# The last three queries put off, and attention's gathers held to the fourth maximum of a step

## The chip, the cores and the metric

The kernel runs on one core of a Trainium2 chip. The metric is the device time of one launch in microseconds (us), lower is better. All numbers are float32.

## The reference

64 sequences of 64 tokens with 512 features pass four layers, each added to its input: x = x + layer(x).

- Layer 0: a dense layer of 512 x 512 whose weight and bias are picked for each sequence out of 16.
- Layer 1: a dense layer of 512 x 512, the same for all, and a rank-16 adapter picked for each sequence out of 8.
- Layer 2: attention against a cache of keys and values. q has 8 heads, k and v have 4, of 64 features. q and k are normed (root mean square over the 64 features of a head, with a learned gain) and rotated by the position. k and v are written into a paged cache at the sequence's position; every query sees the last 256 positions.

```python
q = _rope(_rms(q, q_norm_scale), pos)
...
scores = einsum('bghtd,bgsd->bghts', qg, k_all) * SCALE
p = softmax(where(allowed, scores, -inf), axis=-1)
o = einsum('bghts,bgsd->bghtd', p, v_all)
return einsum('bto,do->btd', o, Wo)
```

- Layer 3: a 64 x 64 product over the tokens of a sequence, with weight and bias picked out of 8.

## The kernel before

**Tiles and phases.** The 4096 tokens are 32 tiles (NT) of 128 tokens, two sequences each. The engines' orders are written out by hand: each engine runs its instructions in the order in which the Python program names them, and semaphores join the engines. The first phase (to about 519 us of the span) does layers 0 and 1 for all tiles, the keys and values (stored to `kvd` in DRAM), and the queries of the first 25 tiles (stored turned to `qTd`). The last eight tiles (LATE) keep their layer-1 output, turned, in SBUF.

**The passage.** In lines 975 to 992 GpSimd starts the gathers of tiles 0 and 1 (`load_kv`), and a loop over tiles 25 to 30 makes their queries: `product` (L140, four float32 matmuls, shown as eight), ScalarE's square (L120), VectorE's sum (L122), ScalarE's root (L123), VectorE's reciprocal and scaling (L126, L128), VectorE's rotation with cosine and sine gains (L133 to L135, the work of `turned`), then `turn_q` (L174: TensorE transposes the query, ScalarE copies it to `qTs`, SP stores it). The query of tile 31 is made in step 0.

**A step.** Then come 32 steps. Step s holds, in this order on each engine:

- GpSimd: `load_kv(s + 2)`: five indirect gathers (L787), 128 rows of 2 KB each, into `kv` (four buffers). In steps 0 and 1 a copy of one element (`after_keys`) makes them wait for the keys of tile s. Then `add_one(s - 2)` (L833), a small sum into the weight `w3`.
- `scores(s)`: 8 products (L860, `ps`), each followed by one VectorE operation that adds the mask, flips the sign and takes the maximum of a row (L868, `mx`; four for the first pair of heads, `gp` 0, then four for the second), and ScalarE's exponential with its sum (L872).
- `attend(s - 1)`: 48 matmuls (L907, `po`), VectorE copies the result (L925).
- `normalise(s, ...)`: VectorE's reciprocals and 8 scalings (L880, L884).
- `last(s - 4)` in even steps from 4 on: layer 3 of two tiles (L947, `pz`; ScalarE L954).
- `project(s - 2)`: the output projection (L935, `py`, in the one bank of pool `pyp`) and VectorE's sum (L939).
- `keys(s + 1)`: TensorE transposes the gathered keys (L841, L847), ScalarE copies them to `kT` (L842, L848).
- `turn(s)`: TensorE transposes the probabilities (L893, L897, `ppt`); VectorE copies two of the five results to `pT` (L894), ScalarE the three others (L894, L898).

All PSUM results but `py` share a ring of seven banks, so a new product waits until the bank used seven allocations earlier has been copied out. The tiles of a `kv` buffer are free again when `attend` has read them, so that a gather for tile i waits for `attend(i - 4)`.

**Who waits.** SP's queue issues the loads of masks, queries, layer-3 weights and the stores in program order. GpSimd's queue is in order as well: what stands behind a waiting gather waits with it.

Of the kernel before, what the change touches and what calls it, by code (L numbers as in the profile page):

```python
# [12 lines left out]
F32 = mybir.dt.float32  # L13
# [36 lines left out]
LATE = 8  # L50
# [9 lines left out]
def body(ctx: ExitStack, tc: tile.TileContext, a: dict, out: bass.AP):  # L60
# [54 lines left out]

    def turned(ps, n, to, pool, X, kind, cg, sg):

        psv = ps[:, : n * HD].rearrange("p (h d) -> p h d", d=HD)
        sq = pool.tile([128, n, HD], F32, name=f"sq{kind}", bufs=2)
        S.activation(sq, psv, AF.Square)  # L120
        ss = pool.tile([128, n], F32, name=f"ss{kind}", bufs=2)
        V.tensor_reduce(ss, sq, AX.X, ALU.add)  # L122
        S.activation(ss, ss, AF.Sqrt, bias=epst, scale=1.0 / HD)  # L123
        yield
        rs = pool.tile([128, n], F32, name=f"rs{kind}")
        V.reciprocal(rs, ss)  # L126
        qn = pool.tile([128, n, HD], F32, name=f"qn{kind}", bufs=2)
        V.tensor_tensor(qn, psv, bc(rs[:, :, None], [128, n, HD]), ALU.mult)  # L128
        yield
        t2 = sq  # L130
        for f in range(2):
            fs, of = slice(f * HALF, (f + 1) * HALF), slice((1 - f) * HALF, (2 - f) * HALF)
            V.tensor_tensor(t2[:, :, fs], qn[:, :, of], bc(sg[:, None, fs], [128, n, HALF]), ALU.mult)  # L133
        V.tensor_tensor(qn, qn, bc(cg[:, None, :], [128, n, HD]), ALU.mult)  # L134
        X.tensor_tensor(to, qn, t2, ALU.add)  # L135
# [6 lines left out]

    def parts_q(i, pq, X, cs=None):
        qr = late.tile([128, H, HD], F32, name="qr", bufs=2)
        qrs[i] = qr.rearrange("p h d -> p (h d)")
        return turned(pq, H, qr, late, X, 0, *(cs or gains(0, i, late, X)))

# [22 lines left out]
    def turn_q(i, pool=late):  # L170
        qrf = qrs.pop(i)
        pqt = bank("pqt")
        for c in range(KC):
            TE.transpose(pqt[:, c * 128 : (c + 1) * 128], qrf[:, c * 128 : (c + 1) * 128], ident)  # L174
        qT = pool.tile([128, 2, 2, 2, T], F32, name="qTs", bufs=2 if pool is late else 4)
# [604 lines left out]

    kvs, kTs, mbs, prs, pTs, oTs, qTs, pairs, x3s = {}, {}, {}, {}, {}, {}, {}, {}, {}

# [8 lines left out]

    def after_keys(i):

        seen = bp.tile([1, 1], F32, name="seen")
        P.tensor_copy(seen, kTs[i][0:1, 0, 0:1])

# [53 lines left out]
    def scores(i):  # L850
        kT, mb, qT = kTs.pop(i), mbs.pop(i), qTs.pop(i)
        pr = bp.tile([128, G, 2 * NPOS], F32, name="pr")
        mx = bp.tile([128, G, 2], F32, name="mx")
        sm = bp.tile([128, G, 2], F32, name="sm")
        for gp in range(2):
            for b2 in range(2):
# [8 lines left out]
                for g2 in range(2):  # L865
# [3 lines left out]
                        out=p, in0=ps[g2][:, :NPOS], in1=mb[:, b2, :], scale=-1.0, scalar=3.0e38,  # L869
                        op0=ALU.add, op1=ALU.min, accum_out=mx[:, g, b2 : b2 + 1],  # L870
                    )
                    S.activation(  # L872
                        p, p, AF.Exp, bias=mx[:, g, b2 : b2 + 1], scale=-1.0, accum_out=sm[:, g, b2 : b2 + 1],
                    )
# [99 lines left out]

    for i in range(2):
        load_kv(i)
    load_q(0)
    load_mask(0)

    parts = {}  # L980
    for i in range(NT - LATE + 1, NT - 1):
        pq = product(i, wq, "pq")
        parts[i] = parts_q(i, pq, V, cs[i])
        next(parts[i])
        if i > NT - LATE + 2:
            turn_q(i - 2, bp)
        if i - 1 in parts:
            run(parts.pop(i - 1))
        next(parts[i])
    keys(0)  # L990
    load_q(1)
    load_mask(1)
    wo = bp.tile([128, KC, D], F32, name="wo", bufs=1)
    for s in range(NT):
        if s + 2 < NT:
            if s < 2:
                after_keys(s)
            load_kv(s + 2)
            load_mask(s + 2)
        if s and s + 2 < NT:  # L1000
            load_q(s + 2)
        scores(s)
        if s >= 2:
            add_one(s - 2)
        if s:
            load_pair(s - 1)
            attend(s - 1)
        else:

            parts[NT - 1] = parts_q(NT - 1, product(NT - 1, wq, "pq", pyp), V, cs[NT - 1])  # L1010
            turn_q(NT - 3, bp)
        if s == 2:
            next(parts[NT - 1])
        normalise(s, 0)
        normalise(s, 1)
        if s % 2 == 0 and s >= 4:
# [79 lines left out]
```

## Time and profile before

| what | value |
|---|---|
| median of 3 runs | 972.71 us (970.54 to 973.45) |
| profiled execution, its own time | 976.14 us |
| its span | 974.3 us |
| granted TensorE clock, mean | 0.995 |
| 0 to 500 us: TensorE busy | 484.42 of 500.00 |
| 545 to 558: TensorE busy, clock | 12.99 of 13.00, 1.00 |
| 558 to 580: TensorE busy, clock | 15.96 of 22.00, 0.84 |
| 580 to 640: TensorE busy, VectorE, ScalarE, GpSimd | 58.01, 43.95, 33.76, 25.60 of 60.00 |
| 820 to 880: the same | 58.32, 43.18, 38.05, 23.21 of 60.00 |
| DMA engines' mean share, 820 to 880 | 0.63 |

Times within the profile count from the span's start. A line such as `kv<-kvd,idxn` names what is written and what is read; in brackets stand the engine's idle time just before and what ended it. Matmuls are pipelined: their starts are measured, their ends modelled.

### The profile page before, as it was taken

What the parts mean: (1) busy time and instruction counts of PE and PEld (TensorE: products, weight loads), DVE (VectorE), ACT (ScalarE), POOL (GpSimd) and SP (SyncE); (2) the same over time, 40 slices, a digit from 0 to 9 for tenths busy, and PEclk for the clock granted to TensorE, in tenths of its full rate; (3) what the DMA queues carried; (4) which work ended last, traced back from release to release, by engine and by line L of the source; (5) the groups of instructions that cost most, each with busy time, mean ns of one, the idle gap of its engine ahead of it and who ended that gap; (6) DMA issues with size and microseconds to landing.
All of it is one profiled execution on the core that took longest, in us unless ns stands there. A gap on an engine that the chain in (4) does not pass through costs nothing.

```text
span 974.3 us, 17800 instructions
## 1 busy us (share of the span) xinstructions
PE 936.3 (96%) x5407; PEld 509.6 (52%) x5407; DVE 608.0 (62%) x1734; ACT 405.2 (42%) x1081; POOL 404.6 (42%) x604
## 2 busy tenths in 40 slices
PE   8899998999999999999999979999999999999998
PEld 3344444444444444444344546766666666666665
DVE  5746788888572353532316768666667776666673
ACT  1212122322232222232223656655566666665663
POOL 4344355554453454534425433334444333334400
PEclk9999999999999999999999989999999999999999
DMA  8898999999999999999854774666665565666621
GB/s 305 306 317 311 358 360 322 395 367 363 381 333 391 393 320 392 359 376 397 310 216 155 241 240 134 205 205 203 204 193 193 177 201 184 190 197 196 198 72 45
DMA packets 132944, 260.74 MB, mean 268 GB/s; under 512 B 32481, under 2 KB 41186, under 8 KB 132850
## 3 DMA queue, kind: packets, MB, share of 16 engines
q1 hardware_dynamic: 108722, 178.74, 51.2%
q0 software_dynamic: 23232, 79.71, 24.6%
q10 hardware_dynamic: 896, 1.16, 0.3%
q8 instruction: 43, 0.70, 0.3%
q14 instruction: 51, 0.42, 0.1%
HBM read 190.06 MB, written 69.50 MB: 266 GB/s over the span
## 4 chain that ended last, share of the span: by engine, by line
PE 70%; DVE 3%; DMA 1%; issue 1%; ACT 1%; SPq 0%; POOL 0%; DVEq 0%; ACTq 0%
PE py L935 12%; PE po L907 8%; PE ps L860 8%; PE p L655 7%; PE pk L140 7%; PE ppt L893 6%; PE pq L140 6%; PE p L266 6%; PE pkt L841 2%; PE ppt L897 2%; PE pkt L847 1%; PE pz L947 1%; DMA w<-in_W 1%; PE pqt L174 1%; DVE pT L894 1%
## 5 line engine op out<-in xcount | busy, mean ns | idle before, releaser
L787 POOL DMA_INDIRECT kv<-kvd,idxn x128 | 126.3, 987 | 216.8 <-PE po L907 159.6
L872 ACT ACTIVATE pr<-pr,mx 128x320 f32<-128x320 f32 x256 | 140.1, 551 | 6.9 <-DVE mx L868 2.6
L266 PE MATMUL p<-w,xt 128*64 128x512 f32 x512 | 122.1, 610 | 1.3 <-DMA w<-in_W 1.3
L935 PE MATMUL py<-wo,oT 128*128 128x512 f32 (+1 forms) x264 | 118.3, 591 | 1.7 <-DVE qn L128 1.7
L140 PE MATMUL pk<-wkv,x 128*128 128x512 f32 x256 | 117.2, 603 | 0.6 <-ACT x L676 0.6
L155 POOL DMA_INDIRECT st<-in_kvc,cidx x68 | 67.3, 990 | 109.2 <-DMA kvd<-st 98.6
L655 PE MATMUL p<-w,x 128*128 128x512 f32 x256 | 112.5, 596 | 0.1
L140 PE MATMUL pq<-wq,x 128*128 128x512 f32 x248 | 111.3, 593 | 0.0
L868 DVE CUSTOM_DVE_ANT_0 pr<-ps,mb 128x320 f32<-128x320 f32 x256 | 107.8, 486 | 5.5 <-PE ps L860 2.7
L860 PE MATMUL ps<-kT,qT 64*128 64x320 f32 x512 | 88.1, 460 | 13.6 <-DVE pT L894 8.5
L894 DVE COPY pT<-ppt 128x512 f32<-128x512 f32 x64 | 41.8, 687 | 77.6 <-PE ppt L893 33.7
L290 DVE TENSOR_TENSOR x<-pt,x 128x512 f32<-128x512 f32 x32 | 22.0, 688 | 107.1 <-PE pt L289 94.7
L884 DVE TENSOR_SCALAR pr<-pr,sm 128x320 f32<-128x320 f32 x256 | 85.2, 394 | 2.2
L907 PE MATMUL po<-pT,kv 128*64 128x128 f32 (+1 forms) x1536 | 84.7, 282 | 1.6 <-issue 1.6
L907 PEld LDWEIGHTS po<-pT,kv 128*64 128x64 f32 (+1 forms) x1536 | 71.0, 138 | 22.3 <-DVE mx L868 13.6
L935 PEld LDWEIGHTS py<-wo,oT 128*128 128x128 f32 x264 | 47.5, 189 | 61.6 <-issue 58.4
L655 PEld LDWEIGHTS p<-w,x 128*128 128x128 f32 x256 | 47.8, 190 | 58.3 <-issue 56.5
L135 POOL TENSOR_TENSOR qr<-qn,sq 128x512 f32<-128x512 f32 x25 | 31.7, 1267 | 109.8 <-DVE qn L134 109.8
L266 PEld LDWEIGHTS p<-w,xt 128*64 128x64 f32 x512 | 35.9, 138 | 71.1 <-issue 65.5
L140 PEld LDWEIGHTS pk<-wkv,x 128*128 128x128 f32 x256 | 46.9, 192 | 49.9 <-issue 48.5
L123 ACT ACTIVATE ss<-ss,epst 128x4 f32<-128x4 f32 (+1 forms) x64 | 19.2, 299 | 125.3 <-DVE ss L122 124.5
L860 PEld LDWEIGHTS ps<-kT,qT 64*128 64x128 f32 x512 | 45.5, 185 | 45.0 <-DVE pT L894 24.0
(200 smaller groups left out, 1344.2 us busy)
## 6 DMA issues: line engine op xcount, KB each, us to landing
w<-in_W SPq DMA_DIRECT2D x62, 1024.0 KB
kvd<-st SPq DMA_DIRECT2D x68, 512.0 KB
xt<-in_xT SPq DMA_DIRECT2D x32, 256.0 KB
x2d<-x2n SPq DMA_DIRECT2D x32, 256.0 KB
kvd<-kvn SPq DMA_DIRECT2D x32, 256.0 KB
qTd<-qTs SPq DMA_DIRECT2D x32, 256.0 KB
qT<-qTd SPq DMA_DIRECT2D x32, 256.0 KB
x2r<-x2d SPq DMA_DIRECT2D x32, 256.0 KB
```

Of the source, the lines that this page charges most:

```text
L140: TE.matmul(ps, x2s[i][:, c, :], w[:, c, :], start=c == 0, stop=c == KC - 1)
L155: P.indirect_dma_start(out=st, out_offset=None, in_=a["kvc"].rearrange("(n r) d -> n (r d)", r=2), in_offset=bass.IndirectOffsetOnAxis(ap= ...
L266: TE.matmul(p0[hs, :], xs[i][:, c, hs], w0s[i][h][:, c, :], start=c == 0, stop=c == KC - 1)
L655: TE.matmul(p1[i], x1s[i][:, c, :], w1[:, c, :], start=c == 0, stop=False)
L787: P.indirect_dma_start(out=kv[:, n, :], out_offset=None, in_=kvd, in_offset=bass.IndirectOffsetOnAxis(ap=at, axis=0),)
L860: TE.matmul(ps[g2][:, :NPOS], qT[rows, gp, b2].rearrange("p h t -> p (h t)"), kT[rows, gp, b2 * NPOS : (b2 + 1) * NPOS], start=True, stop= ...
L868: V.tensor_tensor_reduce(out=p, in0=ps[g2][:, :NPOS], in1=mb[:, b2, :], scale=-1.0, scalar=3.0e38, op0=ALU.add, op1=ALU.min, accum_out=mx[ ...
L872: S.activation(p, p, AF.Exp, bias=mx[:, g, b2 : b2 + 1], scale=-1.0, accum_out=sm[:, g, b2 : b2 + 1],)
L884: V.tensor_scalar(p, p, sm[:, g, b2 : b2 + 1], None, ALU.mult)
L893: TE.transpose(pt[:, n * 128 : (n + 1) * 128], pr[:, g, at : at + 128], ident)
L907: TE.matmul(po[b2][g2 * 64 : (g2 + 1) * 64, gp * 128 : (gp + 1) * 128], kv[rows, n, (G + g) * HD : (G + g + 1) * HD], pT[rows, c, m * 128 ...
L935: TE.matmul(py[:, fs], oT[:, c].rearrange("p b t -> p (b t)"), wo[:, c, fs], start=c == 0, stop=c == KC - 1,)
```

## The change

It has three parts.

- The queries of tiles 29 to 31 (LAST on) are no longer normed and rotated in the passage. ScalarE copies their products out of PSUM into `raw` (the product of 29 between `keys(0)` and `scores(0)`, those of 30 and 31 in steps 0 and 1). GpSimd squares them in steps 2 to 4, VectorE sums the squares in steps 3 to 5, ScalarE takes all three roots in step 6 and runs one exponential behind them, VectorE takes the reciprocal, GpSimd scales and rotates in steps 7 to 12, and `turn_q` follows in steps 9, 11 and 13. The rotation of tile 28 moves from VectorE to GpSimd.
- The gathers of three tiles (15, was 10) start ahead of the passage's loop. From step 1 on `load_kv(s + 2)` stands behind `scores(s)` and behind a one-element copy that reads the fourth maximum (`after_scores`); the maxima get one tile for each pair of heads, so that the copy waits for the first four operations alone. `after_keys` goes.
- GpSimd's other work of a step, `add_one` and the squares and rotations, stands behind the gathers. `qTs` has three buffers in the passage where it had four.

```diff
-    def turned(ps, n, to, pool, X, kind, cg, sg):
+    def turned(ps, n, to, pool, X, kind, cg, sg, M=V):
...
-            V.tensor_tensor(t2[:, :, fs], qn[:, :, of], bc(sg[:, None, fs], [128, n, HALF]), ALU.mult)
-        V.tensor_tensor(qn, qn, bc(cg[:, None, :], [128, n, HD]), ALU.mult)
+            M.tensor_tensor(t2[:, :, fs], qn[:, :, of], bc(sg[:, None, fs], [128, n, HALF]), ALU.mult)
+        M.tensor_tensor(qn, qn, bc(cg[:, None, :], [128, n, HD]), ALU.mult)
...
-    def after_keys(i):
+    def after_scores(i):
 
         seen = bp.tile([1, 1], F32, name="seen")
-        P.tensor_copy(seen, kTs[i][0:1, 0, 0:1])
+        P.tensor_copy(seen, mxs[i][0][0:1, 1, 1:2])
...
-        mx = bp.tile([128, G, 2], F32, name="mx")
+        mxs[i] = [bp.tile([128, 2, 2], F32, name=f"mx{gp}") for gp in range(2)]
...
-    for i in range(2):
+    for i in range(3):
         load_kv(i)
...
+    def keep_raw(i, pq):
+        S.copy(raw[:, i - LAST].rearrange("p h d -> p (h d)"), pq)
+
+    def rotate_raw(i, part):
+        x, t2, (cg, sg) = raw[:, i - LAST], sqr[:, (i - LAST) % 2], cs[i]
+        if part == 0:
+            P.tensor_tensor(x, x, bc(ssr[:, i - LAST, :, None], [128, H, HD]), ALU.mult)
+            for f in range(2):
+                fs, of = slice(f * HALF, (f + 1) * HALF), slice((1 - f) * HALF, (2 - f) * HALF)
+                P.tensor_tensor(t2[:, :, fs], x[:, :, of], bc(sg[:, None, fs], [128, H, HALF]), ALU.mult)
+        else:
+            P.tensor_tensor(x, x, bc(cg[:, None, :], [128, H, HD]), ALU.mult)
+            P.tensor_tensor(x, x, t2, ALU.add)
+            qrs[i] = x.rearrange("p h d -> p (h d)")
...
-    for i in range(NT - LATE + 1, NT - 1):
-        pq = product(i, wq, "pq")
-        parts[i] = parts_q(i, pq, V, cs[i])
+    for i in range(NT - LATE + 1, LAST):
+        X = P if i == LAST - 1 else V
+        parts[i] = parts_q(i, product(i, wq, "pq"), X, cs[i], X)
...
+    run(parts.pop(LAST - 1))
     keys(0)
+    keep_raw(LAST, product(LAST, wq, "pq"))
+    turn_q(LAST - 2, bp)
     load_q(1)
     load_mask(1)
...
         if s + 2 < NT:
-            if s < 2:
-                after_keys(s)
-            load_kv(s + 2)
             load_mask(s + 2)
         if s and s + 2 < NT:
             load_q(s + 2)
         scores(s)
+        if s and s + 2 < NT:
+            after_scores(s)
+            load_kv(s + 2)
         if s >= 2:
             add_one(s - 2)
+        if 2 <= s <= 4:
+            x = raw[:, s - 2]
+            P.tensor_tensor(sqr[:, s % 2], x, x, ALU.mult)
+        elif 7 <= s <= 12:
+            rotate_raw(LAST + (s - 7) // 2, (s - 7) % 2)
         if s:
             load_pair(s - 1)
             attend(s - 1)
-        else:
-            parts[NT - 1] = parts_q(NT - 1, product(NT - 1, wq, "pq", pyp), V, cs[NT - 1])
-            turn_q(NT - 3, bp)
-        if s == 2:
-            next(parts[NT - 1])
+        if s < 2:
+            keep_raw(LAST + 1 + s, product(LAST + 1 + s, wq, "pq", pyp))
+        elif s == 6:
+            S.activation(ssr, ssr, AF.Sqrt, bias=epst, scale=1.0 / HD)
+            S.activation(ssr1, ssr[:, 0, :1], AF.Exp, scale=-1.0)
         normalise(s, 0)
         normalise(s, 1)
+        if s == 6:
+            V.reciprocal(ssr, ssr)
...
-        if s in (4, 5):
-            turn_q(NT - 6 + s, bp)
-        elif s in (2, 3):
-            run(parts.pop(NT - 4 + s))
+        if s == 1:
+            turn_q(LAST - 1, bp)
+        elif s in (9, 11, 13):
+            turn_q(LAST + (s - 9) // 2, bp)
+        elif 3 <= s <= 5:
+            V.tensor_reduce(ssr[:, s - 3], sqr[:, (s - 3) % 2], AX.X, ALU.add)
         turn(s)
...
-        elif s == 1:
-            next(parts[NT - 1])
```

More of the change, by code (lines that the diff above doesn't have):

```diff
@@ L141, in product, with parts_q @@
         return ps
-    def parts_q(i, pq, X, cs=None):
+    def parts_q(i, pq, X, cs=None, M=V):
         qr = late.tile([128, H, HD], F32, name="qr", bufs=2)
         qrs[i] = qr.rearrange("p h d -> p (h d)")
-        return turned(pq, H, qr, late, X, 0, *(cs or gains(0, i, late, X)))
+        return turned(pq, H, qr, late, X, 0, *(cs or gains(0, i, late, X)), M)
     def copies(to, pool, ahead):
@@ L174, in turn_q @@
             TE.transpose(pqt[:, c * 128 : (c + 1) * 128], qrf[:, c * 128 : (c + 1) * 128], ident)
-        qT = pool.tile([128, 2, 2, 2, T], F32, name="qTs", bufs=2 if pool is late else 4)
+        qT = pool.tile([128, 2, 2, 2, T], F32, name="qTs", bufs=2 if pool is late else 3)
         for gp in range(2):
@@ L779, in body @@
     bp = ctx.enter_context(tc.tile_pool(name="bp", bufs=2))
-    kvs, kTs, mbs, prs, pTs, oTs, qTs, pairs, x3s = {}, {}, {}, {}, {}, {}, {}, {}, {}
+    kvs, kTs, mbs, prs, mxs, pTs, oTs, qTs, pairs, x3s = {}, {}, {}, {}, {}, {}, {}, {}, {}, {}
     def load_kv(i):
@@ L869, in scores @@
                         out=p, in0=ps[g2][:, :NPOS], in1=mb[:, b2, :], scale=-1.0, scalar=3.0e38,
-                        op0=ALU.add, op1=ALU.min, accum_out=mx[:, g, b2 : b2 + 1],
+                        op0=ALU.add, op1=ALU.min, accum_out=mxs[i][gp][:, g2, b2 : b2 + 1],
                     )
                     S.activation(
-                        p, p, AF.Exp, bias=mx[:, g, b2 : b2 + 1], scale=-1.0, accum_out=sm[:, g, b2 : b2 + 1],
+                        p, p, AF.Exp, bias=mxs[i][gp][:, g2, b2 : b2 + 1], scale=-1.0, accum_out=sm[:, g, b2 : b2 + 1],
                     )
@@ L978, in body @@
     load_mask(0)
+    LAST = NT - 3
+    raw = bp.tile([128, 3, H, HD], F32, name="raw", bufs=1)
+    sqr = bp.tile([128, 2, H, HD], F32, name="sqr", bufs=1)
+    ssr = bp.tile([128, 3, H], F32, name="ssr", bufs=1)
+    ssr1 = bp.tile([128, 1], F32, name="ssr1", bufs=1)
+    def keep_raw(i, pq):
[11 more added lines that the diff above has]
+            qrs[i] = x.rearrange("p h d -> p (h d)")
     parts = {}
-    for i in range(NT - LATE + 1, NT - 1):
-        pq = product(i, wq, "pq")
-        parts[i] = parts_q(i, pq, V, cs[i])
+    for i in range(NT - LATE + 1, LAST):
+        X = P if i == LAST - 1 else V
+        parts[i] = parts_q(i, product(i, wq, "pq"), X, cs[i], X)
         next(parts[i])
```

## The prediction

> **What bounds it now.** I read the page's engine shares first, then the chain that ended last, then the timeline of single steps.
>
> ```profile
> PE 936.3 (96%) x5407; PEld 509.6 (52%) x5407; DVE 608.0 (62%) x1734; ACT 405.2 (42%) x1081; POOL 404.6 (42%) x604
> ...
> PE 70%; DVE 3%; DMA 1%; issue 1%; ACT 1%; SPq 0%; POOL 0%; DVEq 0%; ACTq 0%
> ...
> L787 POOL DMA_INDIRECT kv<-kvd,idxn x128 | 126.3, 987 | 216.8 <-PE po L907 159.6
> ```
>
> TensorE is busy 96% of the span and carries the chain, so only what makes TensorE wait is worth anything. GpSimd's gathers (L787) wait 159.6 us for `po`: they start when attention's product frees a buffer. That sets where in a step the burst of five lies.
>
> The chain gives the step. Start of the output projection in the last five steps:
>
> ```profile
> 902.42 3.63 PE py L935 x8
> ...
> 928.12 3.63 PE py L935 x8
> ...
> 940.73 3.63 PE py L935 x8
> ...
> 952.49 3.63 PE py L935 x8
> ```
>
> The pair of steps 902.42 to 928.12 takes 25.70; the pair 928.12 to 952.49, which does the same TensorE work, takes 24.37. The second pair has no gathers left. The timeline shows why:
>
> ```profile
> 774.20 0.96 POOL L787 DMA_INDIRECT kv<-kvd,idxn  x1 [6.32 <-PE po L907]
> ...
> 778.43 1.91 PE L893 MATMUL ppt<-ident,pr 128*128 128x128 f32 x16
> ...
> 779.35 0.95 POOL L787 DMA_INDIRECT kv<-kvd,idxh  x1 [0.30 <-issue]
> ...
> 781.42 1.29 DVE L894 COPY pT<-ppt 128x512 f32<-128x512 f32 x2 [3.19 <-PE ppt L897]
> ...
> 782.16 1.95 PE L860 MATMUL ps<-kT,qT 64*128 64x320 f32 x12 [0.65 <-DVE pT L894]
> ```
>
> ```profile
> 945.29 1.91 PE L893 MATMUL ppt<-ident,pr 128*128 128x128 f32 x16
> ...
> 945.93 0.69 DVE L894 COPY pT<-ppt 128x512 f32<-128x512 f32 x1 [0.84 <-PE ppt L893]
> ```
>
> Without gathers the first copy of `pT` starts 0.64 after its transposes start; in the step of 778 it starts 2.99 after, 1.12 behind the fifth gather's end (780.30). The other steps that I read show 1.12 to 1.46 the same way. ScalarE's copies wait until the same moment (781.53), so it is no port that VectorE alone uses: what waits is news of TensorE's results. TensorE then lacks a PSUM bank for the third score and stands. From py of step 3 (592.40) to py of step 29 (928.12) there are 13 pairs in 335.7; 13 x 24.37, and 0.9 for two query transposes there, is 317.7. So the steady steps lose 18.0, nearly all in steps without `last`, where the transposes come 1.0 earlier.
>
> The passage loses more. From the first late query product (519.16) to the first output projection (580.58) are 61.4. The TensorE work is 7 products x 3.45, 5 query transposes x 0.44, 3 scores x 2.4, 2 attends x 2.5, 3 keys x 1.1, 2 turns x 2.2: 46.2. Lost: 15.2.
>
> ```profile
> 560.33 1.11 issue
> ...
> 569.29 3.07 DMA w<-in_w3b
> ...
> 574.34 4.57 PE po L907 x48
> ```
>
> Three bursts, 545.57 to 568.94, run almost without a pause through steps 0 and 1. `po` x48 takes 4.57 instead of 2.50: after the waits the granted clock is 0.84 (mean of 558 to 580).
>
> **The change, part by part.** TensorE does the same operations in all; every gain is a wait.
>
> Queries 29 to 31. Two products move into steps 0 and 1, where now one lies in step 0 and step 1 has no filler. VectorE loses three normalisations of 3.7 each (0.69, 0.20, 0.69, 0.75, 0.69, 0.69) and one rotation, 2.1. It gets three reductions of 0.69 and one reciprocal. ScalarE's squares (0.60) become copies (0.59, as L894's); one of them stands ahead of the key copies and waits for a product that precedes the keys anyway. In the new passage I lay down: product 28 ends at 533.7 as now; keys 0 wait for the first tile's gathers (issued by 531.7, landing an estimated 2 later), 0.5; scores 0 near 540, 5 earlier, slower by 0.9 as VectorE's maxima set their pace (3.26 now); step 1 filled by product 31. The first burst has 15 gathers (3 x 6.3 from 525.4, end 544.2), so its tail lies on scores 0: 1 to 2. With 0.5 each in steps 1 and 2 and 0.5 in the product loop, 4 to 6 of the 15.2 stay. Gain 10, bounds 5 and 12. GpSimd's rotation of tile 28 (2 x 0.72, 2 x 1.27, 4.0) is queued behind those 15 gathers, done near 548, and wanted by its transposes at 560.
>
> The hold. Per step GpSimd first waits for the fourth maximum, copies one element (0.18) and gathers. From the step's first score: first maximum +0.84 (934.96, 935.80), fourth ends +2.56, GpSimd's reaction 0.7 (copy at 544.91, gather at 545.57): burst at +3.3, over 6.1 (774.20 to 780.30), end +9.4, release at +10.65. Now the burst starts at +5.4 (774.20 against 768.80) and releases at +12.6. ScalarE's last key copy at 778.67 was still on time, 4.5 after the burst's start; the `pT` due at 779.07 was not. So the time in which TensorE's news stays out (the blind time) becomes about +7.9 to +10.65. In it fall the add of L939, and in a step without `last` the three key copies (due +9.0), not `pT` alone. Key copies take 1.36: done at +12.0, when the next scores start at +11.76. Then three `pT` copies to +13.6, against a bank wanted near +13.7. I estimate 0.5 lost per such step, none where `last` adds 1.0. 13 x 0.5 is 6.5 of the 18.0. Bounds: 0 (all clear) and the 18.0 of now, and above that if the release slips.
>
> Behind GpSimd's wait stand the sum into w3 (0.33) and the new products, all wanted a step later. The gathered tile is wanted by keys of the next step, +8.4 there or +20.2 here, and lands near +11.5: 8 spare.
>
> GpSimd's work in steps 2 to 4 and 7 to 12 (1.27, 2.7 or 2.5) follows the burst. GpSimd arithmetic at 506.6 to 512.3 did not delay ScalarE's squares (508.68, product end 508.5), so I cost it nothing; if it blinded like a gather, 6 x 2 is 12.
>
> Small: three reductions ahead of `pT` (0.69, after a late L939) hold a bank 0.4 each, 1.2; three query transposes put ScalarE's copies (0.65) ahead of `pT`, 0.2 each; the square root in step 6 brings two table loads of 1.28, hidden between the exponentials (end +6.3) and the key copies, where now the same pair sits in step 2. Sum 2. On SP's queue the stores of the last query tiles move to steps 1, 9, 11 and 13, their loads come in steps 26 to 29: nothing. The store's qTs has three buffers for four; the last stores are two steps apart: nothing.
>
> One rule speaks against the steady gain. The row: copies on two engines wait for a burst's end, 2.35 longer than without one. The Trainium skill's SBUF — State Buffer, "SBUF: two separate sides", says that DMA and engine ports do not contend and that PE and ACT never wait on anyone. By that rule the burst's place would not matter, and the sum would be the passage alone, 10.
>
> Another row: gathers issued while L884 ran took 0.95 (775.47) and 1.08 (776.72), against a median of 0.95; the held burst lies on all of L884, so it may lengthen by some 0.3. The same section says that a two-port VectorE operation locks GpSimd out from writing descriptors. If L884 is one, its 2.7 would by that rule delay the release to +13.3, and the steps would be slower than now.
>
> **Sum.** Passage 10, steady 18.0 - 6.5 - 2.0 = 9.5: 19.5 off. The profiled run took 976.14 (span 974.3, 1.8 around it), so about 956.6 for a like run; the median of the three is 972.71, 3.4 below the profiled run, so about 953. I say 954, with 945 to 964 as this case's own range (steady 4 to 16, passage 5 to 12).
>
> **Rivals.** All clear: the release at +10.65 costs TensorE nothing, 18.0 - 2.0 + 11.5 is 27.5: 945. For it: next scores begin at +11.76. Against: ScalarE has six copies to do between.
>
> Moved, not removed: the hold trades late `pT` for late `kT` at the same loss; the passage alone stays: 972.7 - 9 is about 964. For it: kT feeds the next scores directly.
>
> A wash: the first burst of 15 and late key copies give back the passage as well: within 3 of 972.7.
>
> Slower: the release comes late. If the blind time stretches to +12.5 (gathers lengthened under L884, or a block of 3.1 as at 558.4 to 561.46), key copies end at +13.9: a step without `last` loses 2.05, one with it 1.1, so 3.15 a pair against 1.4: 13 x 1.8 is 23 more, less 9: 987. It decides from a release near +12.1 on, where the steps' extra eats the passage's gain. Against it: ten gathers from 525.4 to 538.7 lie beside the product loop with waits of 0.8 at most.
>
> **Chances.** Forecast 0.56; all clear 0.12; moved 0.10; wash 0.06; slower 0.16. Faster by over 0.3% (2.9, about what a measurement of this kernel can tell) is 0.78, within it 0.06, slower 0.16. The range runs from 940, 5 below the all-clear case for its unknown passage, to 974, which holds the wash; outside it lie the slower case and a few hundredths below.
>
> **What would show it.** Right: the first L787 of a step follows the fourth maximum by under 1, its release precedes `pT`; steps of a pair add up to 24.4 to 25.2; granted clock 1.0 from 558 to 580; the first output projection near 570. Wrong: key copies (L842) 2 or more behind their transposes with TensorE waiting at the first scores; pairs still near 25.7; gathers well above 0.95; a wait of products or scores 0 in 534 to 546 of over 3.

## The result, and the profile after

| | median | lowest to highest | runs |
|---|---|---|---|
| before | 972.12 us | 970.54 to 973.45 | 4 |
| changed | 1027.79 us | 1026.96 to 1032.03 | 4 |

The ratio is 1.0582, with an interval of 1.0557 to 1.0607: 56 us slower, where 18.7 faster was forecast. The profiled run of the changed kernel has a span of 1025.2, that of before 974.3: 50.9 between them (before's profiled run took 976.14, 4.0 above its median of four, the changed one 1026.96, 0.8 below its own).

On some occasions the kernel before has a median of 971 to 977, as here, and on others of 950 to 951, with the same code and the same data; I call the first the late place and the second the prompt place.

The page of the changed kernel, to be laid beside that of before:

```profile
PE 958.2 (93%) x5407; PEld 522.5 (51%) x5407; DVE 603.8 (59%) x1713; ACT 405.1 (40%) x1080; POOL 429.8 (42%) x653
...
PE 64%; DVE 8%; another core or an unknown queue 2%; DMA 1%; issue 1%; ACT 1%; SPq 0%; POOL 0%; ACTq 0%
...
L893 PE MATMUL ppt<-ident,pr 128*128 128x128 f32 x512 | 82.8, 309 | 35.0 <-DVE pr L884 34.9
...
L925 DVE COPY oT<-po 128x256 f32<-128x256 f32 x64 | 25.1, 421 | 150.2 <-PE pkt L847 52.4
```

TensorE's share of the chain fell from 70% to 64%, VectorE's rose from 3% to 8%. The transposes of the probabilities (L893) stood 35.0 for VectorE's scalings (L884), a wait that was not among before's large ones. The last line is the clue: `oT`, the copy of attention's product `po`, is put down as waiting for `pkt`, the key transposes, a product made long after `po`. A copy that waits for something younger than its source has not been told that its source is done. I call this telling, from one engine to another, news. One step of the timeline shows it:

```profile
828.48 2.56 PE L907 MATMUL po<-pT,kv 128*64 128x128 f32 x48
...
828.72 0.18 POOL L795 COPY seen<-mx 1x1 f32<-1x1 f32 x1 [5.40 <-DVE mx L868]
...
829.44 0.99 POOL L787 DMA_INDIRECT kv<-kvd,idxn  x1 [0.54 <-issue]
...
830.97 3.70 PE L935 MATMUL py<-wo,oT 128*128 128x512 f32 x8
...
834.50 0.94 POOL L787 DMA_INDIRECT kv<-kvd,idxh  x1 [0.30 <-issue]
...
836.75 0.76 DVE L925 COPY oT<-po 128x256 f32<-128x256 f32 x2 [6.52 <-PE pkt L847]
...
837.06 0.86 ACT L842 COPY kT<-pkt 128x384 f32<-128x384 f32 x2 [5.14 <-PE pkt L847]
...
837.63 1.27 DVE L884 TENSOR_SCALAR pr<-pr,sm 128x320 f32<-128x320 f32 x4
...
838.07 1.33 PE L893 MATMUL ppt<-ident,pr 128*128 128x128 f32 x8 [1.87 <-DVE pr L884]
```

`po` ends at 831.04. The burst of five gathers runs from 829.44 to 835.44, starting under `po`. VectorE stands until 1.3 after it and ScalarE until 1.6: `oT` starts 5.7 after its product's end. Behind `oT` in VectorE's order stand the scalings, so the transposes lack their input and TensorE stands 1.87. In most of the other steps without layer 3 (`last`) the first copy of `oT` came 5.6 to 6.0 late, behind the burst. In nine of the 13 steps with it the copy came 2.1 to 2.8 late, within the burst; in three it came 5.8 to 5.9 late and in one 1.6. The chain of waits has the same stretch in another step:

```profile
801.91 6.72 another core or an unknown queue
...
808.66 0.76 DVE oT L925 x2
```

No other core runs; the line means that the profile found no releaser for 6.72.

The sum of the 50.9, by landmarks on TensorE's timeline (start of the 32 key products `pk` of the first phase, first output projection, `po` of step 3, `po` of step 29):

| stretch | before | changed | difference |
|---|---|---|---|
| to `pk` | 504.88 | 505.98 | +1.1 |
| `pk` to the first projection (passage) | 75.70 | 71.67 | -4.0 |
| to `po` of step 3 | 9.26 | 12.44 | +3.2 |
| 13 pairs of steps, `po` 3 to `po` 29 | 335.72 | 381.69 | +46.0 |
| to the end of the span | 48.70 | 53.42 | +4.7 |

So the passage gained and the steady steps lost. TensorE's work in the 13 pairs, as windows of both kernels (columns: window and length, then busy time of TensorE, its weight loads, VectorE, ScalarE, GpSimd, granted clock, DMA share, GB/s). Before:

```profile
589.84:925.56 335.72, 325.78 (x2767) 219.95 (x2765) 232.21 (x811) 208.87 (x603) 135.48 (x156) 1.00 0.61 193
```

Changed:

```profile
590.09:971.78 381.69, 347.30 (x2770) 234.98 (x2768) 239.33 (x811) 212.76 (x610) 154.95 (x199) 0.96 0.58 169
```

Idle TensorE grew from 9.9 to 34.4, and its busy time by 21.5, at a granted clock of 0.96. So each wait shows twice: as idle time and as slower work behind it. Behind the wait shown above, from 838.00 to 841.50, the granted clock was 0.69.

### The profile page after: what moved, and what is told of

Its sections match the earlier page's. It is cut to its first block, busy times and chain, and to the rows that moved or that the text cites. A ratio compares the mean times of both kernels' runs of the same rounds, so it can differ in the third digit from the quotient of the medians.

```text
span 1025.2 us, 17830 instructions
## 1 busy us (share of the span) xinstructions
PE 958.2 (93%) x5407; PEld 522.5 (51%) x5407; DVE 603.8 (59%) x1713; ACT 405.1 (40%) x1080; POOL 429.8 (42%) x653
## 3 DMA queue, kind: packets, MB, share of 16 engines
q1 hardware_dynamic: 108722, 178.74, 49.7%
## 4 chain that ended last, share of the span: by engine, by line
PE 64%; DVE 8%; another core or an unknown queue 2%; DMA 1%; issue 1%; ACT 1%; SPq 0%; POOL 0%; ACTq 0%
PE py L935 10%; PE ps L860 7%; PE po L907 7%; PE p L655 7%; PE pk L140 6%; PE pq L140 6%; PE ppt L893 6%; PE p L266 5%; DVE pr L884 3%; PE pkt L841 2%; PE pkt L847 2%; PE ppt L897 1%; DVE oT L925 1%; PE pz L947 1%
## 5 line engine op out<-in xcount | busy, mean ns | idle before, releaser
L787 POOL DMA_INDIRECT kv<-kvd,idxn x128 | 124.1, 969 | 51.5 <-issue 44.5
L893 PE MATMUL ppt<-ident,pr 128*128 128x128 f32 x512 | 82.8, 309 | 35.0 <-DVE pr L884 34.9
L925 DVE COPY oT<-po 128x256 f32<-128x256 f32 x64 | 25.1, 421 | 150.2 <-PE pkt L847 52.4
L140 PE MATMUL pq<-wq,x 128*128 128x512 f32 x240 | 107.7, 593 | 0.0
L884 DVE TENSOR_SCALAR pr<-pr,sm 128x320 f32<-128x320 f32 x256 | 93.2, 426 | 2.2
L795 POOL COPY seen<-mx 1x1 f32<-1x1 f32 x29 | 5.2, 179 | 204.9 <-DVE mx L868 204.9
L893 PEld LDWEIGHTS ppt<-ident,pr 128*128 128x128 f32 x512 | 62.4, 155 | 54.2 <-DVE pr L884 34.5
L860 PE MATMUL ps<-kT,qT 64*128 64x320 f32 x512 | 84.1, 455 | 4.3 <-issue 3.4
L907 PE MATMUL po<-pT,kv 128*64 128x128 f32 (+1 forms) x1536 | 82.3, 278 | 0.2 <-issue 0.2
L907 PEld LDWEIGHTS po<-pT,kv 128*64 128x64 f32 (+1 forms) x1536 | 68.9, 135 | 19.8 <-DVE mx L868 13.6
```

The lines of the kernel that those rows point to most:

```text
L140: TE.matmul(ps, x2s[i][:, c, :], w[:, c, :], start=c == 0, stop=c == KC - 1)
L787: P.indirect_dma_start(out=kv[:, n, :], out_offset=None, in_=kvd, in_offset=bass.IndirectOffsetOnAxis(ap=at, axis=0),)
L860: TE.matmul(ps[g2][:, :NPOS], qT[rows, gp, b2].rearrange("p h t -> p (h t)"), kT[rows, gp, b2 * NPOS : (b2 + 1) * NPOS], start=True, stop= ...
L884: V.tensor_scalar(p, p, sm[:, g, b2 : b2 + 1], None, ALU.mult)
L893: TE.transpose(pt[:, n * 128 : (n + 1) * 128], pr[:, g, at : at + 128], ident)
L907: TE.matmul(po[b2][g2 * 64 : (g2 + 1) * 64, gp * 128 : (gp + 1) * 128], kv[rows, n, (G + g) * HD : (G + g + 1) * HD], pT[rows, c, m * 128 ...
```

## The experiments

Theory P: the place of the burst. In the late place TensorE's completions (its news that a result is done) reach the other engines late while GpSimd gathers; the held burst lies over `po`, so `oT` and all that VectorE and ScalarE do behind it wait for the burst's end. Rival D: the put-off queries are the cost. Later rivals: A, every gather costs the same wherever it lies; E, the late place is slow in itself; G, the gain of spread gathers comes from elsewhere; B, C and S are told below.

### The parts apart

No hold (e1): the change, with the gathers at the head of the step as before, from step 1 on.

```diff
+            if s:
+                load_kv(s + 2)
         scores(s)
-        if s and s + 2 < NT:
-            after_scores(s)
-            load_kv(s + 2)
```

> The change with the put-off queries, but without the hold: the five gathers stand at the head of a step and start when attention's product frees a buffer, as in the kernel before. Theory P (place): while a burst of gathers runs, TensorE's completions reach the other engines late, and the held burst lies over the end of attention's product, so that its copies wait. Then this kernel's pairs of steps are back at 25.5 to 25.8 us, no copy of oT starts over 0.1 after its product, and the passage keeps the 4 us that it gained: 966 to 971. Rival D (deferral): the squares and rotations on GpSimd, the extra table loads and the later transposes cost the time: it stays above 1010.

Hold alone (e2): the kernel before, with the hold from step 2 on and nothing else.

```diff
             if s < 2:
                 after_keys(s)
-            load_kv(s + 2)
+                load_kv(s + 2)
             load_mask(s + 2)
...
         scores(s)
+        if 2 <= s < NT - 2:
+            after_scores(s)
+            load_kv(s + 2)
```

The maxima are split in two tiles here as well, as `after_scores` needs it.

> The kernel before with nothing but the hold: from step 2 on the gathers stand behind the fourth maximum. Theory P: oT is copied 2 to 6 us late in steps 2 to 29 and the time is 1020 to 1030, the passage as in the kernel before. Rival D: within 5 of 972.

Hold on `oT` (e3): the change, the one-element copy reads `oT` instead of the maximum.

```diff
-        if s and s + 2 < NT:
-            after_scores(s)
-            load_kv(s + 2)
+        if s:
+            load_pair(s - 1)
+            attend(s - 1)
+            if s + 2 < NT:
+                seen = bp.tile([1, 1], F32, name="seen")
+                P.tensor_copy(seen, oTs[s - 1][0:1, 0, 1, 0:1])
+                load_kv(s + 2)
...
-        if s:
-            load_pair(s - 1)
-            attend(s - 1)
```

> The change, with the gathers held as well, but to the copy of attention's result (oT) instead of the fourth maximum; they start some 2.3 us later in the same step, where those of the kernel before lie, with one step less of lead. Theory P: the place within the step decides: pairs of 25.5 to 25.8, pT late by 2 as before, 966 to 973. A rival L (lead): a gather that is asked for a step later comes too late for its keys: TensorE waits at L841, over 1000. Rival D: above 1010.

No gathers (e4): the change, tiles 4 to 31 reuse the keys and values of the first four tiles and gather nothing.

```diff
-        kv = kvs[i] = kvp.tile([128, 5, 2 * G * HD], F32, name="kv")
+        if i >= 4:
+            kvs[i] = held[i % 4]
+            return
+        kv = kvs[i] = held[i] = kvp.tile([128, 5, 2 * G * HD], F32, name="kv")
```

This kernel leaves out the keys and values of tiles 4 to 31 and is there for its time alone.

> The change with the gathers of tiles 4 to 31 left out: those tiles use the keys and values of the first four. Every wait for the fourth maximum stays, with nothing behind it. Theory P: no burst, no late news: pairs of 24.3 to 24.6, 947 to 955. Rival D: the steps 2 to 13 keep their loss, above 985.

| run | median | ratio to before, run beside them (951.00) |
|---|---|---|
| no hold | 947.77 | 0.9958 [0.9939, 0.9977] |
| hold alone | 949.79 | 0.9984 [0.9971, 0.9997] |
| hold on `oT` | 948.60 | 0.9975 [0.9965, 0.9985] |
| no gathers | 947.84 | 0.9966 [0.9944, 0.9987] |

Three of the four forecasts missed, for the same reason: here the kernel before took 951.00, and the hold cost nothing. The fourth, no gathers, fell within its 947 to 955, but so did every version here. These runs can't tell P from D. They showed that the 56 us were not a property of the code alone. Hold on `oT` was run only here, so what it takes in the late place is not known.

### The change again

No edit. The theories are S (late news belongs to the occasion) and C (only all parts together bring it).

> The change itself, once more, beside the kernel before. In the first comparison the kernel before took 972 and the change 1028; in the second session the kernel before took 951 and none of four variants showed a late copy. Theory S (place and session): the late news of TensorE during gathers is a property of the chip or session on which a run falls; where the kernel before takes about 951 it is absent, and the change takes 944 to 949 there, oT copied within 0.2 of its product. Where the kernel before takes about 972 the change takes over 1015. Rival C (combination): hold and put-off queries together make the late news, which neither makes alone: then 1010 or more beside a kernel before of 951.

Measured: 948.25 against 950.95, ratio 0.9971 [0.9956, 0.9986]. S held and C fell: the very kernel that took 1027.79 took 948.25. A step of it, in the timeline:

```profile
773.65 2.56 PE L907 MATMUL po<-pT,kv 128*64 128x128 f32 x48
...
774.82 0.99 POOL L787 DMA_INDIRECT kv<-kvd,idxn  x1 [0.54 <-issue]
...
776.25 0.76 DVE L925 COPY oT<-po 128x256 f32<-128x256 f32 x2 [0.64 <-PE po L907]
...
779.88 0.95 POOL L787 DMA_INDIRECT kv<-kvd,idxh  x1 [0.30 <-issue]
...
780.26 0.86 ACT L842 COPY kT<-pkt 128x384 f32<-128x384 f32 x2 [2.96 <-PE pkt L841]
```

The burst lies over `po` exactly as in the first profile (1.17 after its start, there 0.96) and its gathers take the same time (0.99 for the first, 0.95 for the last), but `oT` starts 0.04 after `po` ends. The same program, the same overlap, no lateness.

### More gathers, where nothing was late

Hold alone and no hold once more (the edits above), and the hold alone with every gather of tiles 4 to 31 made twice (h1):

```diff
+            if i >= 4:
+                dump = kvp.tile([128, 2 * G * HD], F32, name="dump", bufs=4)
+                P.indirect_dma_start(
+                    out=dump, out_offset=None, in_=kvd,
+                    in_offset=bass.IndirectOffsetOnAxis(ap=at, axis=0),
+                )
```

> The kernel before with the hold alone, from step 2 on, once more, because the first time of it came where the kernel before took 951 and no copy of the attention product stood late. Theory P (the place of the burst: where TensorE's completions come late during gathers, a burst that lies over the attention product holds up its copies) expects: if the kernel before takes about 972 here, 1015 to 1030 and copies 5 to 6 us late in most steps; if the kernel before takes about 951, 948 to 952 and copies 0.0 to 0.2 late. Rival D (the queries put off are the cost, where completions come late): within 8 of the kernel before in either case.

> The change without the hold (gathers at the head of the step from step 1 on, as before), again beside it. P: if the kernel before takes about 972, 963 to 970; if about 951, 946 to 950. D: if the kernel before takes about 972, over 1010; if about 951, 946 to 950.

> The hold alone, with every gather of tiles 4 to 31 made twice, the second time into a spare buffer that nobody reads: ten gathers of 0.97 us in a burst, some 9.7 us, of a step of 12.2. Theory B (the late news is a matter of how much GpSimd gathers at once, and the other sessions only lay under a threshold) expects the copies of the attention product 2 us late or more in most steps and 990 or above. Theory S (it belongs to where the kernel ran, not to the amount) expects, where the kernel before takes about 951, copies 0.0 to 0.2 late and a time within 8 of the hold alone; GpSimd then has about 11.5 us of work in a step of 12.2, so it does not become the bound.

Before 950.54; hold alone 949.01 (0.9986 [0.9968, 1.0004]); no hold 948.96 (0.9988 [0.9961, 1.0014]); doubled gathers 971.20 (1.0208 [1.0158, 1.0258]). With ten gathers a step the first copy of `oT` started 0.03 to 0.04 after its product, so theory B (a threshold in the amount) falls. The 20 us that they cost are another matter, and the expectation of S, within 8 of the hold alone, missed it: between 580 and 920 us its waits have `PEld pz L958 <- POOL w L844: 17.3, 12, 1.5`, layer 3's weight sum, queued on GpSimd behind ten gathers.

### The late place met again

Hold alone, one run:

> The hold alone a third time, for the session: theory S (late news belongs to where and when the kernel runs) expects 948 to 952 with copies of the attention product 0.0 to 0.2 late if the kernel before takes about 951, and, if the kernel before takes about 972, by the place of the burst 1015 to 1030 with copies 5 to 6 us late. Rival D (the queries put off are the cost where news is late): within 8 of the kernel before in either case.

Measured: 1037.95, the kernel before beside it 976.57, one run of each, so more than P's 1015 to 1030. D falls: with not one query put off, the hold alone costs 61. Its timeline:

```profile
863.53 2.56 PE L912 MATMUL po<-pT,kv 128*64 128x128 f32 x48
...
864.76 0.99 POOL L787 DMA_INDIRECT kv<-kvd,idxn  x1 [0.54 <-issue]
...
872.33 0.76 DVE L930 COPY oT<-po 128x256 f32<-128x256 f32 x2 [6.78 <-PE pkt L852]
```

`oT` starts 6.24 after `po` ends. The last three products of the same run, which have no gathers left beside them, are copied 0.03 after their end.

The rest was run next, and met the prompt place: no hold and no gathers (edits above), and the change with its burst taken apart, one gather behind each of five events (s1). `load_part` copies one element of the tile that it is given and starts one gather:

```diff
-            after_scores(s)
-            load_kv(s + 2)
+        load_part(s + 2, 0, mxs[s][0][0:1, 1, 1:2])
+        load_part(s + 2, 1, mxs[s][1][0:1, 1, 1:2])
...
             attend(s - 1)
+            load_part(s + 2, 2, oTs[s - 1][0:1, 0, 1, 0:1])
...
             keys(s + 1)
+            load_part(s + 2, 3, kTs[s + 1][0:1, 0, 0:1])
...
         turn(s)
+        load_part(s + 2, 4, pTs[s][0:1, 0, 0:1])
```

> The change without the hold, for a place where completions come late during gathers (there the kernel before takes about 972 to 977, and the hold alone took 1037.95). Theory P, the place of the burst: the rest of the change is harmless, so 962 to 971 there. Rival D, the queries put off are a cost of their own there: over 985. Where the kernel before takes about 951, both expect 946 to 950.

> The change with the gathers of tiles 4 to 31 left out (those tiles attend to the keys and values of the first four), the waits of GpSimd kept. Theory P and its ground, that completions come late only while GpSimd gathers: where the kernel before takes about 972 to 977, copies of the attention product 0.0 to 0.1 late from step 3 on, pairs of steps 24.4, and 946 to 957. Rival E, that place is slower in itself (clock, memory) and the hold only adds a wait: over 965 there. Where the kernel before takes about 951, both expect 946 to 950.

> The change with its burst of five gathers taken apart: one gather each behind the fourth maximum, the eighth maximum, the copy of the attention product, the first copy of the keys and the first copy of the probabilities. If a completion is late by what is left of an unbroken burst (theory P), a single gather of 0.97 can hold news up by about 1 us: where the kernel before takes about 972 to 977, 950 to 965 and no copy over 2 late. If each gather costs the same wherever it lies (rival A), no better than the kernel before. Where the kernel before takes about 951: 946 to 952.

Before 950.36; no hold 946.21 (0.9963 [0.9935, 0.9992]); no gathers 948.56 (0.9981 [0.9940, 1.0023]); spread 947.88 (0.9973 [0.9949, 0.9996]). As expected there, and nothing told apart. So each was run again by itself.

Spread:

> The spread version again, for a place where the kernel before takes about 972 to 977. Theory P (a completion is late by what is left of an unbroken burst): 950 to 965 there, no copy over 2 late. Rival A (each gather costs the same wherever it lies): no better than the kernel before. Where the kernel before takes about 951: 946 to 950 by both.

Measured, in two runs: 958.68 against 970.97, ratio 0.9868 [0.9835, 0.9900]. The late place, and P against A: the same gathers cost the 13 pairs 4 us instead of 63 (table below). `oT` was 0.1 to 2.0 late. In one step four gathers ran together again (878.46 to 883.46, gaps of 0.3 to 0.4), TensorE stopped within `po`, and that step took 15.90 instead of 11.75. So nearly all of the 4 us that are left come from this one step, in which the gathers were a burst again.

No hold:

> The change without the hold once more, for a place where the kernel before takes about 972 to 977. Theory P (the hold's place is the whole cost): 962 to 971 there. Rival D (the queries put off cost there too): over 985. Where the kernel before takes about 951: 944 to 950 by both.

Measured: 973.19 against 977.23, ratio 0.9961 [0.9943, 0.9978]; the late place again. D is refuted a second time (P's 962 to 971 was too low, the kernel before being at 977 and not at the 972 that P set out from). The late news is still there, but it finds other work:

```profile
743.25 0.76 DVE L925 COPY oT<-po 128x256 f32<-128x256 f32 x2 [0.95 <-PE po L907]
...
743.55 0.96 POOL L787 DMA_INDIRECT kv<-kvd,idxn  x1 [6.96 <-PE po L907]
...
747.27 0.86 ACT L842 COPY kT<-pkt 128x384 f32<-128x384 f32 x2 [3.21 <-PE pkt L841]
...
748.71 0.95 POOL L787 DMA_INDIRECT kv<-kvd,idxh  x1 [0.30 <-issue]
...
750.97 1.29 DVE L894 COPY pT<-ppt 128x512 f32<-128x512 f32 x2 [3.39 <-PE ps L860]
```

The burst starts when `oT` has just been copied; `kT` is on time 3.7 into it; only `pT` waits for its end. Here, as in the kernel before, the gathers wait for the news of `po` themselves, so that their burst can't hold up `oT`. The hold took this order away.

No gathers:

> The change with the gathers of tiles 4 to 31 left out (those tiles attend to the keys and values of the first four tiles), the waits of GpSimd kept, for a place where the kernel before takes about 972 to 977. Theory P with its ground, that completions come late only while GpSimd gathers: copies of the attention product 0.0 to 0.1 late from step 3 on, pairs of steps 24.4, and 950 to 960 (the passage and the first phase stay as there). Rival E, that place is slower in itself and GpSimd's waits on the maximum are the cost: over 985. Where the kernel before takes about 951: 946 to 950 by both.

> The change without the gathers of tiles 4 to 31 (those tiles attend to the keys and values of the first four), once more for a place where the kernel before takes about 972 to 977. Theory P with its ground (completions come late only while GpSimd gathers): copies of the attention product 0.0 to 0.1 late from step 3 on, pairs of steps 24.4, and 950 to 960. Rival E (the place is slower in itself, GpSimd's waits are the cost): over 985. Where the kernel before takes about 951: 946 to 950 by both.

The first met the prompt place: 948.08 against 950.46, ratio 0.9970 [0.9952, 0.9988]. The second met the late one, in two runs: 954.42 against 973.64, ratio 0.9801 [0.9731, 0.9872], and the same windows line as above reads:

```profile
586.25:904.56 318.31, 318.31 (x2770) 223.08 (x2768) 234.34 (x811) 214.27 (x609) 28.97 (x69) 1.00 0.35 98
```

TensorE busy 318.31 of 318.31, with GpSimd's waits kept. E falls: without gathers the 13 pairs of the late place take what they take in the prompt one (318.32). In the one held step of this run that still gathers, step 1, news is late:

```profile
560.06 2.56 PE L912 MATMUL po<-pT,kv 128*64 128x128 f32 x48
...
560.69 1.02 POOL L792 DMA_INDIRECT kv<-kvd,idxn  x1 [0.16 <-issue]
...
565.77 0.95 POOL L792 DMA_INDIRECT kv<-kvd,idxh  x1 [0.30 <-issue]
...
567.74 0.76 DVE L930 COPY oT<-po 128x256 f32<-128x256 f32 x2 [5.81 <-PE pkt L852]
```

### The passage by itself

The kernel before with spread gathers (n2: the same five places, from step 2 on) beside the change with spread gathers:

> The kernel before with only its gathers taken apart (one each behind the fourth maximum, the eighth, the copy of the attention product, the first copy of the keys, the first copy of the probabilities; from step 2 on). Theory P expects the steady loss of 18 nearly gone where the kernel before takes about 972 to 977: 957 to 963, and the passage's loss kept, 3 to 6 above the change with spread gathers in the same call. Where the kernel before takes about 951: 948 to 952, 2 to 3 above it. Rival G (the gain of the spread version came from the passage and the put-off queries, not from the gathers): within 4 of the kernel before in either case.

> The change with spread gathers once more, beside the kernel before with spread gathers, for what the put-off queries and the third early tile are worth with the gathers' place taken out: theory P expects 955 to 961 where the kernel before takes about 972 to 977, 946 to 949 where it takes about 951.

Before 976.18; before with spread gathers 961.34 (0.9834 [0.9802, 0.9866]); the change with spread gathers 962.12 (0.9848 [0.9815, 0.9882]). The late place. P's 957 to 963 held and G fell. P's 955 to 961 for the change was missed by 1, and P's 3 to 6 between the two versions are not there: beside spread gathers, the put-off queries and the third early tile were worth nothing that these runs can tell. The passage of the kernel before, from the 32 key products `pk` to the first output projection, gained from the spread too: it took 70.81, where it takes 75.70 with bursts, and that of the change 71.34. Both profiles have, at the same place, the step in which gathers ran together and `po` stopped (5.1 instead of 2.56).

All together, the 13 pairs of steps of each profile, which the prediction put at 317.7 without loss (the doubled gathers left out):

| kernel | late place | prompt place |
|---|---|---|
| before | 335.72 | no profile taken |
| no hold | 334.84 | 318.10 |
| hold alone | 386.87 | 317.66 |
| the change | 381.69 | 318.32 |
| the change, spread gathers | 322.57, 322.94 | 318.31 |
| before, spread gathers | 323.61 | not run |
| hold on `oT` | not run | 318.10 |
| no gathers | 318.31 | 318.32 |

The right column moves by 0.7 at most; the left one moves with the place of the gathers alone by 59 in the change (381.69 to 322.57) and by 63 in the kernel before (386.87 to 323.61), and without them it reads as the right one.

## Why the prediction was wrong

**What held.** The reading of before: transposed probabilities late by a burst, 18.0 in 13 pairs, the floor of 317.7 (measured without gathers 318.31). The new burst's place: forecast +3.3 to +9.4 from the step's first score with the release at +10.65; in the step shown, first score 825.92, it was +3.52, +9.52 and +10.83. That rival "slower" was wrong in its mechanism, then: the release did not come late.

**The step that failed** is the start of the blind time: "the time in which TensorE's news stays out becomes about +7.9 to +10.65". I took from one row that news gets through for the first 4.5 us of a burst, because in before a key copy 4.5 after its start was on time, and moved that figure along with the burst. But in before the first 4.5 us lie over the output projection, eight long matmuls; in the new place they lie over `po`, 48 short ones. There the blind time began no later than 1.6 after the burst's start (829.44 to 831.04), and took in `oT`. So I priced late key copies and `pT`, at 0.5 per step without `last`, and never priced `oT`, behind which stand VectorE's scalings and TensorE's transposes. In the kernel before no burst could hold `oT` up in the steady steps: its gathers waited for `po` themselves. The true term was +46.0 where the sum had -9.5. A figure for how long a resource stays open had been read under one neighbour, and was used under another.

The profile of before had a row for the new neighbour. In its step 1, within the passage, a burst lies over `po`:

```profile
554.35 0.98 POOL L787 DMA_INDIRECT kv<-kvd,idxn  x1 [0.16 <-issue]
...
557.77 1.78 PE L907 MATMUL po<-pT,kv 128*64 128x128 f32 x27
...
559.38 0.94 POOL L787 DMA_INDIRECT kv<-kvd,idxh  x1 [0.30 <-issue]
...
560.03 0.29 PE L907 MATMUL po<-pT,kv 128*64 128x128 f32 x1 [0.48 <-issue]
...
561.43 1.08 PE L907 MATMUL po<-pT,kv 128*64 128x128 f32 x20 [1.11 <-issue]
```

`po` stopped after 27 matmuls and went on for good 1.11 after the burst's end (560.32). The prediction names this block (558.4 to 561.46) only as a way in which the release could come late, in its rival "slower", and not as what happens to `po` under a burst.

**Why then 1.6 and not 4.5?** Not settled. A guess is that `po` sends many completions in a short time and the long matmuls few; that `po` itself stopped in the rows above, and in the spread versions where four gathers ran together, would fit it. A pause between two gathers lets news in: in step 5 of the changed kernel none ran from 623.00 to 624.22, and `oT` was copied at 623.70, 1.57 late. The guess does not say why the news came within the burst in most steps with layer 3, where eight more matmuls lie between `po` and the output projection. No run changed the number of matmuls under a burst.

**The passage**: forecast 10, with bounds 5 and 12. Measured by landmarks, the gain is 4.0 in the late place, 75.70 to 71.67 (70.36 without the hold), below the lower bound. In the prompt place it is 2.0, 66.76 (hold alone, which has the passage of before) to 64.77. The mis-sized term is the tail of the 15 gathers on scores 0, "1 to 2":

```profile
540.48 1.88 PE L860 MATMUL ps<-kT,qT 64*128 64x320 f32 x10
...
545.07 0.58 ACT L988 COPY raw<-pq 128x512 f32<-128x512 f32 x1 [5.12 <-remote]
...
545.14 0.94 POOL L787 DMA_INDIRECT kv<-kvd,idxh  x1 [0.30 <-issue]
...
545.71 1.41 PE L860 MATMUL ps<-kT,qT 64*128 64x320 f32 x2 [3.36 <-issue]
...
547.19 0.65 ACT L177 COPY qTs<-pqt 128x256 f32<-128x256 f32 x2 [1.53 <-PE ps L860]
...
547.88 2.01 PE L860 MATMUL ps<-kT,qT 64*128 64x320 f32 x4 [0.76 <-PE ps L860]
...
547.91 0.49 DVE L868 CUSTOM_DVE_ANT_0 pr<-ps,mb 128x320 f32<-128x320 f32 x1 [8.45 <-PE ps L860]
```

Scores 0 began where forecast, near 540, and ended at 549.9: they took 9.4 where 3.3 and a tail of 1 to 2 had been priced. The new copy of `raw`, which I had costed at nothing, started 5.0 after its product's end (540.11), still within the burst. The copy of a query behind it (`qTs`) came 1.1 after the burst's end (546.08) and the first maximum 1.8 after it. TensorE lacked banks meanwhile: it went on at 545.71 and 547.88, just after these two copies had ended (545.65 and 547.84). In step 1 `oT` came 4.9 late as well. The clock granted from 545 to 560 was 0.77.

In the prompt place another term was mis-sized. GpSimd's rotation of tile 28 was costed as harmless; there it runs beside VectorE's scalings:

```profile
542.22 2.88 DVE L884 TENSOR_SCALAR pr<-pr,sm 128x320 f32<-128x320 f32 x4
...
543.24 1.68 POOL L133 TENSOR_TENSOR sq<-qn,sg 128x256 f32<-128x256 f32 x2
...
545.23 3.16 DVE L884 TENSOR_SCALAR pr<-pr,sm 128x320 f32<-128x320 f32 x4
```

Four scalings take 1.27 in the changed kernel's step shown above (837.63), here 2.88 and 3.16, and the next scores follow at 549.71. In step 0 of the hold alone, in the prompt place and without that rotation, they take 1.44 and 1.27.

**The rule of the Trainium skill**, SBUF — State Buffer, "SBUF: two separate sides", says that DMA and engine ports do not contend and that PE and ACT never wait on anyone. The prediction drew from it that the burst's place would not matter. That came out in the prompt place (`oT` 0.04 late under a burst, the 13 pairs within 0.7 in the table) and not in the late one, where the measurement decides. The rule speaks of ports, and what came late was news; no run shows by which way news goes, so that the rule itself is wrong about the ports is not shown. A lock-out of gathers by L884 was not seen in either place: the 86 gathers of before that ran beside it have a median of 0.96 us, the other 74 of 0.95, and in the prompt step shown (773.65) those beside it took 0.94 to 0.96.

**What was outside the profile.** The traces of before come from the late place alone. Nothing in them told that the same kernel also runs in 951, with no late news at all. Where f1 ran, the change was 0.3% faster than the kernel before.

## What to carry to other kernels

How long a burst on one engine leaves the others undisturbed belongs to what runs beside it: when a burst is moved, read the row of its new neighbours, and ask of every consumer there what stands behind it. Short pieces spread over the step are safer than one burst in a well chosen place: taken apart behind five events, the gathers gave 0.983 to 0.987 of before where news was late (959 to 962 against 971 to 976), the lowest times of any version there that does the whole work, and about 0.997 (947.88) where it was not. Before a loss is explained from one trace, run the unchanged kernel again elsewhere.

## What the runs showed of the hardware

- One program has two times, 950 to 951 and 971 to 977. In the steps the extra is late news of TensorE's results during GpSimd's gathers: in the late place the 13 pairs take 335.72 in the kernel before and, without the gathers of tiles 4 to 31, 318.31. The gathers themselves are the same in both (mean of L787 969 ns in the changed kernel's late profile, 976 in its prompt one). The late place was met with four chip numbers (2, 8, 11, 15) and the prompt one with four (4, 9, 11, 14); that of the first comparison is not on record. One number was seen in both, so the number does not decide. What does is open.
- In the late place, under a held burst, VectorE's copy of `oT` starts up to 6.2 after the product's end and, in most steps without layer 3, 1.2 to 1.6 after the burst's; ScalarE's key copy starts 0.3 after it in such steps (836.75 and 837.06 above).
- In the late place TensorE itself stopped within `po` where a burst lay over it in step 1 of before, and went on 1.11 after the burst's end.
- Beside GpSimd's rotation VectorE's scalings take more than twice as long (2.88 and 3.16 for four against 1.27).
- A wait costs TensorE twice: in the 13 pairs 24.4 more idle and 21.5 more busy. Of the busy time, the transposes behind the wait (L893) carry most: 68.6 against 49.7 in before, while the output projections stay at 96.7 against 96.2.
